# Output projections in 64x128 array tiles over four banks, and context values of both batches at once

## The chip, the cores and the metric

The kernel runs on one core of a Trainium2 chip. The metric is the device time of one launch in microseconds (us). A core has a matrix engine (TensorE, PE in the profile, with PEld for its weight loads), a vector engine (VectorE, DVE), an activation engine (ScalarE, ACT), a general one (GpSimd, POOL) and a queue that issues transfers (SyncE, SP). Each works through its own list of instructions in order and waits on semaphores for the others. PE writes into PSUM, eight banks of 128 rows by 512 fp32 numbers, and the other engines have to empty them.

## The reference

A transformer block on `x` (2 batches, 1024 tokens, 256 features) with a context of 2 x 154 rows of 192 features, all in fp32:

```
h = layernorm(x, ln1);  x = x + attention(h, h, sa_*)        # 16 heads of 64
h = layernorm(x, ln2);  x = x + attention(h, context, ca_*)  # 154 keys
h = layernorm(x, ln3);  p = h @ ff_w1 + ff_b1
x = x + (p[:, :1024] * gelu(p[:, 1024:])) @ ff_w2 + ff_b2
```

`attention` projects queries, keys and values to 1024 features, takes a softmax over the keys, weighs the values and projects the result back to 256 features with `wo`, adding `bo`.

## The kernel before

The work is cut into units: a unit is one batch and one pair of heads (8 pairs, 16 units a stage). There are three stages. Self-attention runs over 128 positions, eight a unit. The context stage ("ca", the loop `for c in range(CA)`) runs over 48 steps, three a unit: the counter `n` is 0, 1, 2, and a step handles 3, 3 and 2 tiles of 128 tokens. Steps are counted from 0, so that step 10 is n = 1 of unit 3. The feed-forward follows. Nothing is reordered behind the program: the order in which the code emits instructions is the order of each engine.

A step of the context stage does this. `cross_first` has PE compute the scores `sc` of its token tiles (K is 64, so the two heads of a pair run in the two row halves of the array) and DVE their negated maxima `neg`. ACT takes exponentials with their sums, three for each head in a step of three tiles. One step later, DVE takes reciprocals `rden` and POOL multiplies. Two steps later (`cross_drain`), DVE transposes the result into `pT_ca`.

Beside this, each n has its own work:

- n = 0: `cross_values` weighs the context values for the unit two before, over all four free banks (`poc`). DVE and ACT copy them out into `o_ca`, DVE's part emitted ahead of its transposes.
- n = 1: `cross_queries` projects the queries `pq_ca` of the next unit into the two main banks; ACT copies them out at the next step.
- n = 2: output projection, context values, and one turn of a norm.

The eight banks are four for scores (two buffers of two), two main ones (`mm_tile`) and two for sums (`sum_tile`). Each of the two small pools hands its banks out in turn.

The output projection takes two head pairs (`HP`) at a time, a group; a batch has four groups. `out_piece` computes two token tiles in one bank with full-array matmuls (`py_ca`, `py_sa`), and DVE adds them to `x`. Four pieces make a group. They are kept in `outs` and taken by `run_work`. Self-attention already uses another form, `out_rounds`: four token tiles in four banks. Each K of 128 is split into its two row halves, which run at once into two different banks and are then exchanged. Before the exchange ACT reads one element of a bank (`seen`) so that both halves are through. There the matmuls are cut into 64x32 tiles. The last self-attention group falls into the context stage and goes by `out_piece`.

The norms of the next stage are prepared beside. `norm_beside` puts pieces into `side`: pieces of statistics, deviation and normalization (DVE `st_ln`, `mv_ln`, `off_ln`; POOL `rstd_ln`, `xn_ln`) alternate with pieces of a turn, four transposes on PE (`ph_ln`) that DVE or ACT then stores into `home`. A turn needs a bank. `run_work` takes the pieces in their order and stops at a turn when it has no bank to give; it had one at n = 2 only. Context-attention's norm of batch 1 turns in units 3 to 6, the feed-forward's norm of batch 0 in units 12 to 15.

`context_values` computes the 128 first context rows' values for one batch and two head pairs: two fp32 matmuls with 96 rows each (an fp32 matmul is two instructions in the trace), an ACT copy into `own_v`, and a transfer to DRAM and back that spreads them to four partition groups (`vd`). It is called for even units, eight times.

Of the kernel before, what the change touches and what calls it, by code (L numbers as in the profile page):

```python
# [18 lines left out]
def tile_transformer_block(ctx: ExitStack, tc: tile.TileContext, a: dict, out: bass.AP):  # L19
# [127 lines left out]
    def load_weights(kind, pr, what):  # L147
        if kind == "sa" and what == "v":
            wsl[kind, pr, what], parts = load_slice(f"{kind}_w{what}", pr * P, VC, HR)
            return parts  # L150
        elif kind == "sa" or what == "q":
            wsl[kind, pr, what] = load_slice(f"{kind}_w{what}", pr * P, P, HR)
        elif pr % 2 == 0:
            wsl[kind, pr, what] = load_slice(f"{kind}_w{what}", pr * P, VC, CC)

# [379 lines left out]

    def out_rounds(b, g, tiles):

        o = oT["sa", b, g]
# [20 lines left out]
        def add(at):  # L559
            t = tiles[at]  # L560
            xs = xt[b, t // GT][:, t % GT, :]
            nc.vector.tensor_tensor(xs, py[at][:, :D], xs, ALU.add)
            added.add(("sa", b, g, t))

        for pair in range(2):
            cross(pair, 0)
        return [lambda pair=pair: second(pair) for pair in range(2)], [
            lambda at=at: add(at) for at in range(4)]

    def out_order(kind):  # L570
# [237 lines left out]

    held, kept, rounds = [], [], []

    def self_beside(ui):
# [15 lines left out]
        if ui >= HP and ui % HP == 0:  # L827
            ob, og = divmod(ui // HP - 1, NQ)
            for t0 in range(0, NG * 2, 2):
                rounds.append(  # L830
                    (ob, og, [t + e for t in out_order("sa")[t0:t0 + 2] for e in range(2)]))
        if ui in (4, 6):
            add_biases("sa", (ui - 4) // 2)

    coming, ahead_ends = [], []
    to_dram = [(1, 3), (1, 6), (3, 3)]
    from_dram = [(NU - 1, n) for n in (0, 3, 5)]

    def load_ahead(p):
# [17 lines left out]
        if ahead_ends and (ui == 1 and n == SH + 1 or ui == 2 and n in (0, 1, SH)):  # L857
            ahead_ends.pop(0)()
        if (ui, n) in to_dram:
            i = 2 * to_dram.index((ui, n))  # L860
# [92 lines left out]

    def context_values(b, pr, bank=mm_tile):

        v = vs["ca", b, pr // 2] = pt_.tile([P, NB, VC], F32, tag="V", name=f"v_ca{b}_{pr}")
        pv = bank(f"pv_ca{b}_{pr}")
        for c in range(2):  # L960
            nc.tensor.matmul(
                pv[:, :VC], lhsT=ctxT[:, c, b * TP:b * TP + P],
                rhs=wsl["ca", pr, "v"][:, c, :], start=(c == 0), stop=(c == 1),
            )

        def store():
            own = one.tile([P, VC], F32, tag="own_v", name=f"own_v{b}_{pr}")
            nc.scalar.copy(own, pv[:, :VC])
            later.insert(0, lambda: nc.sync.dma_start(out=vd[b, pr][:P, :], in_=own))

            def back(a0):
                for a4 in range(a0, a0 + 2):
                    nc.sync.dma_start(
                        out=v[a4 * KB:(a4 + 1) * KB, :, :],
                        in_=vd[b, pr].rearrange("(n p) d -> p n d", p=KB))

            later.insert(2, lambda: back(0))
            later.insert(3, lambda: back(2))

        return store  # L980
# [8 lines left out]
    def cross_first(c):  # L989
# [18 lines left out]

        def then(between=None):
            pr_ = pp_.tile([P, 2, TG, NB * KB], F32, tag="P", name=f"p_{c}")  # L1010
            nc.gpsimd.memset(pr_[:, :, :, T:], 0.0)
            den = small.tile([P, 2, TG], F32, tag="den", name=f"den_{c}")
            for j in range(2):
                if j and between:
                    between()
                for i in range(nt):
# [62 lines left out]
    def cross_beside(ui):  # L1079
# [3 lines left out]
        if ui > HP and ui % HP == 1:  # L1083
            out_pieces("ca", *divmod(ui // HP - 1, NQ), out_order("ca"))
        if ui == NU - 5:
# [238 lines left out]
    with tc.manual_schedule():  # L1324
# [53 lines left out]
        side.append((True, (), lambda: together(*(lambda b=b: turn_context(b) for b in range(B)))))  # L1378
        side.append((True, (), turn_rows))
        work.append(costing(2, lambda: self_queries(*units[0], P, 2 * P)))  # L1380
        work.extend(value_pieces(0, (mm_tile, sum_tile)))
        work.append(costing(2, lambda: three_keys(0)))

        for p in range(SA):
# [23 lines left out]
            if p < 2 * SH - 1 or p % SH in (1, 2):  # L1408
# [9 lines left out]
                elif p == SA - 2:  # L1418
                    hold_late_keys()
                    run(lambda: context_values(*units[0]))  # L1420
                    for pr in range(NKD, NPAIR):
# [7 lines left out]
        for c in range(CA):  # L1429
# [5 lines left out]
            if c == SH:  # L1435
                out_pieces("sa", B - 1, NQ - 1, out_order("sa"))
# [4 lines left out]
            ui, n = divmod(c, len(CG))  # L1441
            nxt = units[ui + 1] if ui + 1 < NU else None
            if n == 0:
# [3 lines left out]
            elif n == 2 and nxt and ui:  # L1447
                load_weights("ca", nxt[1], "v")
            flush(adds)
            between = None  # L1450
            if c < 2:
# [5 lines left out]
            if c < 2:  # L1457
                weighted(SA + c - 2, 0)
                weighted_beside(SA + c - 2, 1)
                if c == 0:  # L1460
                    slot[SA - 1]["dd"] = differences(SA - 1, slot[SA - 1]["st"])
                    between = lambda: softmax_join(SA - 1)
# [134 lines left out]
```

## Time and profile before

| | us |
|---|---|
| median of 3 runs | 1060.7 (1059.21 to 1061.69) |
| the profiled execution | 1060.44 |
| its span | 1058.6 |
| PE busy | 1047.1 |
| DVE busy | 880.7 |
| POOL busy | 769.9 |
| ACT busy | 658.9 |
| `py_ca`, 256 instructions | 61.1 |
| `pv_ca`, 32 instructions | 8.5 |

A row of the timeline is start, length, engine, line, operation, out<-in, shape and count. In a matmul's shape "64*128" is the tile of the array, "64x256" rows by moving columns. Matmuls are pipelined, so that the length of one is more than its distance to the next. A row of groups ends with busy time, the mean of one in ns, and the engine's idle time ahead of it with what ended it. A row of stretches gives for PE, PEld, DVE, ACT and POOL the busy time and the count, then the granted clock of PE, the share of the DMA engines and GB/s.

### The profile page before, as it was taken

The page shows a single profiled execution, that of the slowest core. Times are in us where ns is not written, and L with a number is a line of the kernel's source. Part 1 is how long each engine was busy: PE and PEld are TensorE (multiplying, and loading weights), DVE is VectorE, ACT ScalarE, POOL GpSimd, SP SyncE. Part 2 cuts the span into 40 slices and gives each one's busy share as a digit, 9 for nine tenths or more (in the row PEclk, how much of TensorE's full clock was granted, in tenths as well). Part 3 has the DMA queues.
Part 4 walks back from the last instruction along what each step waited for, and adds up shares of the span by engine and source line. Part 5 has one row for each costly group of instructions (what it writes and reads, how often), then busy time and mean ns, then how long its engine had stood idle before and what let it go on. Part 6 is the DMA issues. An engine that isn't in the chain of part 4 may idle for free.

```text
span 1058.6 us, 51303 instructions
## 1 busy us (share of the span) xinstructions
PE 1047.1 (99%) x21700; PEld 740.3 (70%) x21700; DVE 880.7 (83%) x1313; ACT 658.9 (62%) x2147; POOL 769.9 (73%) x1620
## 2 busy tenths in 40 slices
PE   8999999999999999999999999999999999999998
PEld 6456965556576666665786676666676667889997
DVE  5799999999899999999999999968776777675654
ACT  5776767777776766766776777666666655243221
POOL 2677777788778777777777777757665777598773
PEclk9999999999999999999999999999999999999999
DMA  4322221121121021122122012135323221000000
GB/s 106 95 65 60 50 61 42 45 54 34 25 54 45 15 54 45 29 44 55 24 44 50 21 39 56 49 104 132 101 59 83 69 59 41 1 11 11 21 11 30
DMA packets 96023, 52.87 MB, mean 50 GB/s; under 512 B 30314, under 2 KB 93810, under 8 KB 95794
## 3 DMA queue, kind: packets, MB, share of 16 engines
q1 hardware_dynamic: 94466, 48.93, 18.9%
q8 instruction: 171, 2.80, 1.1%
q10 hardware_dynamic: 1328, 0.66, 0.2%
q14 instruction: 58, 0.48, 0.1%
HBM read 36.23 MB, written 4.39 MB: 38 GB/s over the span
## 4 chain that ended last, share of the span: by engine, by line
PE 90%; DVE 4%; ACT 2%; POOL 2%; issue 1%; DMA 1%; SPq 0%; DVEq 0%; POOLq 0%; ACTq 0%
PE s L583 20%; PE po L639 20%; PE pv_sa L443 5%; PE py_ca L523 5%; PE pk_sa L411 5%; PE pq_sa L411 5%; PE pr L547 5%; PE pf L1289 5%; PE poc L1064 4%; PE pb L1169 4%; PE pq_ca L411 4%; PE sc L999 3%; PE pa L1169 2%; PE pc L1169 2%; PE ph_ln L323 1%
## 5 line engine op out<-in xcount | busy, mean ns | idle before, releaser
L600 ACT ACTIVATE p<-s,st 128x512 f32<-128x512 f32 x512 | 345.4, 685 | 152.8 <-DVE st L592 121.4
L706 POOL TENSOR_SCALAR p<-p,rd,ee 128x512 f32<-128x512 f32 x508 | 385.2, 768 | 75.5 <-DVE rd L698 75.1
L592 DVE TENSOR_REDUCE st<-s 128x2 f32<-128x1024 f32 x256 | 308.7, 1207 | 49.9 <-issue 16.1
L733 DVE STREAM_TRANSPOSE pT<-p 128x1024 f32<-128x1024 f32 x256 | 303.9, 1221 | 2.4 <-POOL p L706 2.3
L583 PE MATMUL s<-k_sa,q_sa 64*32 64x512 f32 x4096 | 256.7, 590 | 1.1 <-DVE k_sa L432 0.6
L639 PE MATMUL po<-pT,v_sa 64*32 64x256 f32 x6144 | 180.5, 376 | 1.7 <-ACT p L1017 1.6
L639 PEld LDWEIGHTS po<-pT,v_sa 64*32 64x32 f32 x6144 | 142.7, 106 | 45.0 <-issue 15.2
L583 PEld LDWEIGHTS s<-k_sa,q_sa 64*32 64x32 f32 x4096 | 102.8, 106 | 78.5 <-issue 51.4
L1017 ACT ACTIVATE p<-sc,neg 128x154 f32<-128x154 f32 x256 | 97.1, 406 | 72.2 <-DVE rden L1025 70.2
L1028 POOL TENSOR_SCALAR p<-p,rden 128x154 f32<-128x154 f32 x256 | 96.8, 399 | 52.9 <-DVE rden L1025 51.9
L600 ACT ACTIVATION_READ_ACCUMULATOR p<-s,st 128x1 f32 x512 | 103.0, 201 | 0.0
L1004 DVE TENSOR_REDUCE neg<-sc 128x6 f32<-128x924 f32 (+1 forms) x48 | 48.1, 1003 | 20.2 <-PE sc L999 20.0
L523 PE MATMUL py_ca<-ca_wo,o_ca 128*128 128x256 f32 x256 | 61.1, 385 | 0.0
L639 PE MATMUL po<-pT,third_v 64*32 64x256 f32 x2048 | 60.5, 376 | 0.0
L443 PE MATMUL pv_sa<-sa_wv,home 64*32 64x256 f32 x2048 | 60.2, 376 | 0.0
L443 PEld LDWEIGHTS pv_sa<-sa_wv,home 64*32 64x32 f32 x2048 | 48.4, 106 | 14.1 <-issue 5.4
L411 PE MATMUL pq_sa<-home,sa_wq 64*32 64x512 f32 (+1 forms) x976 | 58.0, 586 | 0.0
L411 PE MATMUL pq_ca<-home,ca_wq 64*128 64x512 f32 (+1 forms) x352 | 57.8, 589 | 0.0
L639 PEld LDWEIGHTS po<-pT,third_v 64*32 64x32 f32 x2048 | 46.6, 106 | 16.0 <-issue 4.6
L1017 ACT ACTIVATION_READ_ACCUMULATOR p<-sc,neg 128x1 f32 x256 | 56.5, 221 | 0.0
L627 POOL TENSOR_TENSOR zz<-ee,st 128x8 f32<-128x8 f32 x128 | 25.8, 202 | 42.1 <-ACT ee L625 42.1
L411 PE MATMUL pk_sa<-home,sa_wk 64*32 64x512 f32 x960 | 56.3, 589 | 0.0
(144 smaller groups left out, 1576.1 us busy)
## 6 DMA issues: line engine op xcount, KB each, us to landing
st<-st SPq DMA_DIRECT2D x510, 1.0 KB, 1.7
v_sa<-v_sa SPq DMA_DIRECT2D x24, 256.0 KB, 3.3
v_ca<-vd SPq DMA_DIRECT2D x32, 160.0 KB, 3.4
sa_wq<-in_L_xattn_sa_wq_dram SPq DMA_DIRECT2D x32, 128.0 KB, 3.3
sa_wk<-in_L_xattn_sa_wk_dram SPq DMA_DIRECT2D x32, 128.0 KB, 3.1
sa_wv<-in_L_xattn_sa_wv_dram SPq DMA_DIRECT2D x32, 128.0 KB, 3.3
ca_wq<-in_L_xattn_ca_wq_dram SPq DMA_DIRECT2D x32, 128.0 KB, 3.0
wf<-in_L_xattn_ff_w_dram SPq DMA_DIRECT2D x12, 256.0 KB, 4.8
```

Source lines behind the costliest of these rows:

```text
L411: nc.tensor.matmul(pq[r][f:f + m, at:at + n], lhsT=wt[own, c, f:f + m], rhs=h[own, c, t0:t0 + n], start=(c == 0), stop=(c == NH - 1), tile ...
L443: nc.tensor.matmul(pv[r][f:f + KB, i * VC:(i + 1) * VC], lhsT=h[own, c, t0:t0 + KB], rhs=wt[own, c, :], start=(c == 0), stop=(c == NH - 1) ...
L523: nc.tensor.matmul(py[:, e * D:(e + 1) * D], lhsT=o[:, i, (t + e) * P:(t + e + 1) * P], rhs=wo[kind, b, g][:, i, :], start=(i == 0), stop= ...
L583: nc.tensor.matmul(sc[a4 * KB:(a4 + 1) * KB, j, :], lhsT=q[r, c:c + KB], rhs=k[r, h * HB:(h + 1) * HB], start=True, stop=True, tile_positi ...
L592: nc.vector.tensor_reduce(st[:, 0, 0, i, :], sc, AX.X, ALU.max, negate=True)
L600: nc.scalar.activation(pr[:, j, :], sc[:, j, :], AF.Exp, bias=st[:, 0, 0, i, j:j + 1], accum_out=st[:, 0, 1, i, j:j + 1],)
L639: nc.tensor.matmul(po[a2][d:d + KB, :QH // 2], lhsT=v[r, t, e, d:d + KB], rhs=pT[r, d // DH * NK + n, :], start=(t == 0 and e == 0), stop= ...
L706: nc.gpsimd.tensor_scalar(pr[:, j, :], pr[:, j, :], v["rd"][:, c:c + 1], v["ee"][:, 0, c:c + 1], op0=ALU.mult, op1=ALU.mult,)
L733: nc.vector.transpose(halves[h][:, :, c:c + KB], slot[p]["members"][i].rearrange("p j (n k) -> p (j n) k", k=KB))
L1017: nc.scalar.activation(pr_[:, j, i, :T], sc[:, j, i * T:(i + 1) * T], AF.Exp, bias=neg[:, j, i:i + 1], accum_out=den[:, j, i:i + 1],)
L1028: nc.gpsimd.tensor_scalar(pr_[:, j, i, :T], pr_[:, j, i, :T], rden[:, j, i:i + 1], 1.0, op0=ALU.mult, op1=ALU.mult,)
L1169: nc.tensor.matmul(into[:, :BT], lhsT=lhs, rhs=wh[pair][i], start=first, stop=True, skip_group_check=True)
```

## The change

- `out_rounds` serves both kinds of attention and takes the tile width `m`. The last group of self-attention and all groups of context attention but the last go by rounds with 64x128 tiles. A round runs at n = 2 (at n = 1 too in units 1 and 15), between the scores and the exponentials; ACT's two `seen` reads stand ahead of the exponentials of the first and of the second head. Its four adds go to DVE at the start of the next step.
- The turn of a norm runs at n = 1, between the scores and the queries, in a sum bank. Pieces without a turn still run at n = 0.
- `context_values` handles both batches: the context is copied (eight transfers during self-attention) into `ends`, batch 0 in rows 0 to 63 and batch 1 in rows 64 to 127, three chunks of 64; the weights are loaded into both halves of the rows. It runs at n = 1 of units 2, 4 and 6 in two sum banks, and once at the end of self-attention in two main banks. Batch 1 loads no value weights and no longer projects; it fetches its spread values.
- `poc` takes the sum banks first in some units.

```diff
-    def out_rounds(b, g, tiles):
+    def out_rounds(kind, b, g, tiles, m=KB):
...
-                for f in range(0, P, KB):
+                for f in range(0, P, m):
                     for r in (1, 0):
                         at = 2 * pair + (r ^ swapped)
                         own, t0 = slice(r * HR, (r + 1) * HR), tiles[at] * P + f
                         nc.tensor.matmul(
-                            py[at][f:f + KB, :D], lhsT=o[own, i, t0:t0 + KB],
-                            rhs=wo["sa", b, g][own, i, :],
+                            py[at][f:f + m, :D], lhsT=o[own, i, t0:t0 + m],
+                            rhs=wo[kind, b, g][own, i, :],
...
+    def four_by_four(kind, b, g):
+
+        pairs = out_order(kind)
+        for i in range(0, len(pairs), 2):
+            rounds.append((kind, b, g, [t + e for t in pairs[i:i + 2] for e in range(2)]))
...
+    def context_values(pr, bank):
+        v = hold_values(0, pr)
+        pv = [bank(f"pv_ca{b}_{pr}") for b in range(B)]
+        for c in range(DC // HR):
+            for b in range(B):
+                own = slice(b * HR, (b + 1) * HR)
+                nc.tensor.matmul(
+                    pv[b][:, :VC], lhsT=both_ctx[own, c, :], rhs=wsl["ca", pr, "v"][own, c, :],
+                    start=(c == 0), stop=(c == DC // HR - 1), tile_position=(b * HR, 0))
...
             if n == 0 and ui > 1:
-                own, between = cross_values(ui - 2, [mm_tile] * 2 + [sum_tile] * 2)
-                lates.append(then(between))
+                banks = [mm_tile] * 2 + [sum_tile] * 2
+                if side and side[0][0] or ui % 2 == 0 and not b:
+                    banks.reverse()
+                own, copy = cross_values(ui - 2, banks)
+                lates.append(then([copy]))
                 own()
             else:
+                if n == 1 and ui:
+                    spare["turned"] = True
+                    if ui % 2 == 0 and not b:
+                        run(lambda: context_values(ui, sum_tile))
+                    run_work(0, 1, sum_tile)
+                    flush(stores)
+                if rounds and (n == 2 or n == 1 and (ui == 1 or not nxt)):
+                    between, taken = out_rounds(*rounds.pop(0), P)
                 lates.append(then(between))
...
             elif n == 1:
-                spare["turned"] = True
-                if ui == 1 or not nxt:
-                    run_work(2, 0)
-                else:
+                if ui > 1 and nxt:
                     run(lambda: cross_queries(*nxt))
-                run_work(0, 1)
             else:
-                run_work(0, 0, n_sum=1)
-                flush(adds)
-                if ui and ui % 2 == 0:
-                    run(lambda: context_values(*units[ui]))
-                run_work(0, 1, mm_tile)
-                flush(stores)
-                if ui > 1:
-                    run_work(0, 0, n_sum=1)
+                if b and ui % 2 == 0:
+                    hold_values(*units[ui])
+                    spread_values(*units[ui], 0)
...
+            adds.extend(taken)
```

More of the change, by code (lines that the diff above doesn't have):

```diff
@@ L153, in load_weights @@
         elif pr % 2 == 0:
-            wsl[kind, pr, what] = load_slice(f"{kind}_w{what}", pr * P, VC, CC)
+            t = wsl[kind, pr, what] = wpool.tile(
+                [P, DC // HR, VC], F32, tag="wv", name=f"{kind}_w{what}_{pr}")
+            own = w[f"{kind}_w{what}"][:, pr * P:pr * P + VC].rearrange("(c p) f -> p c f", p=HR)
+            for r0 in range(0, P, HR):
+                nc.sync.dma_start(out=t[r0:r0 + HR], in_=own)
     def load_ahead_parts():
@@ L807, in self_first @@
         return then
[L809 removed]
+    held, kept = [], []
     def self_beside(ui):
@@ L828, in self_beside @@
             ob, og = divmod(ui // HP - 1, NQ)
-            for t0 in range(0, NG * 2, 2):
-                rounds.append(
-                    (ob, og, [t + e for t in out_order("sa")[t0:t0 + 2] for e in range(2)]))
+            four_by_four("sa", ob, og)
         if ui in (4, 6):
@@ L952, in context_ends @@
         return store
[L954 to L964, printed above, removed]
-        def store():
[L967 to L978, printed above, removed]
+    both_ctx = ends[:, :DC // HR * P].rearrange("p (c k) -> p c k", k=P)
@@ new lines, in context_beside @@
+    def context_beside():
+        moves = []
+        for b in range(B):
+            for c in range(DC // HR):
+                f = c * HR
+                while f < (c + 1) * HR:
+                    half, row = divmod(f, CC)
+                    n = min((c + 1) * HR - f, CC - row)
+                    to = b * HR + f - c * HR
+                    moves.append(lambda b=b, c=c, half=half, row=row, n=n, to=to: nc.sync.dma_start(
+                        out=both_ctx[to:to + n, c, :],
+                        in_=ctxT[row:row + n, half, b * TP:b * TP + P]))
+                    f += n
+        return moves
@@ new lines, in hold_values, with spread_values, back @@
+    def hold_values(b, pr):
+        v = vs["ca", b, pr // 2] = pt_.tile([P, NB + B, VC], F32, tag="V", name=f"v_ca{b}_{pr}")
+        return v
+    def spread_values(b, pr, at):
+        def back(a0):
+            for a4 in range(a0, a0 + 2):
+                nc.sync.dma_start(
+                    out=vs["ca", b, pr // 2][a4 * KB:(a4 + 1) * KB, :NB, :],
+                    in_=vd[b, pr].rearrange("(n p) d -> p n d", p=KB))
+        later.insert(at, lambda: back(0))
+        later.insert(at + 1, lambda: back(2))
@@ L1007, in cross_first, with then @@
         )
-        def then(between=None):
+        def then(between=()):
             pr_ = pp_.tile([P, 2, TG, NB * KB], F32, tag="P", name=f"p_{c}")
@@ L1013, in then @@
             for j in range(2):
-                if j and between:
-                    between()
+                for fn in between[j:j + 1] if len(between) > 1 else between if j else ():
+                    fn()
                 for i in range(nt):
@@ L1419, in tile_transformer_block @@
                     hold_late_keys()
-                    run(lambda: context_values(*units[0]))
+                    run(lambda: context_values(0, mm_tile))
                     for pr in range(NKD, NPAIR):
@@ L1447, in tile_transformer_block @@
             elif n == 2 and nxt and ui:
-                load_weights("ca", nxt[1], "v")
+                if not nxt[0]:
+                    load_weights("ca", nxt[1], "v")
             flush(adds)
-            between = None
+            between, taken = (), ()
             if c < 2:
```

24 lines of the change are left out of this document (19 added, 5 removed).

## The prediction

> **What bounds the kernel now.** I read the page first, then busy time by stretch, then the timeline of single units in the context stage.
>
> ```profile
> span 1058.6 us, 51303 instructions
> PE 1047.1 (99%) x21700; PEld 740.3 (70%) x21700; DVE 880.7 (83%) x1313; ACT 658.9 (62%) x2147; POOL 769.9 (73%) x1620
> PE   8999999999999999999999999999999999999998
> PEclk9999999999999999999999999999999999999999
> PE 90%; DVE 4%; ACT 2%; POOL 2%; issue 1%; DMA 1%; SPq 0%; DVEq 0%; POOLq 0%; ACTq 0%
> ```
> ```profile
> 760.00:820.00 60.00, 60.00 (x726) 43.13 (x724) 42.77 (x86) 37.54 (x175) 36.36 (x102) 1.00 0.32 81
> ```
>
> The edits act in the context stage (687 to 892 us, 16 units of three steps). There the columns of the second fence (PE, PEld, DVE, ACT, POOL) give PE 60.00 of 60 and DVE 42.77: every microsecond that PE waits is lost, every one of PE work saved is won. The other engines have time to spare, but each runs in order, so what matters is how soon after PE they finish.
>
> **The projections themselves.**
>
> ```profile
> 736.46 1.89 PE L523 MATMUL py_ca<-ca_wo,o_ca 128*128 128x256 f32 x8
> 19.59 2.00 PE L411 MATMUL pq_sa<-home,sa_wq 64*128 64x256 f32 x16
> L961 PE MATMUL pv_ca<-ca_wv,ctxT 96*128 96x256 f32 x32 | 8.5, 388 | 0.3 <-ACT q_ca L426 0.2
> ```
>
> A full-array matmul instruction costs (1.89-0.386)/7 = 0.215 us, 0.386 being the length of one. In 64x128 tiles two run at once: (2.00-0.376)/7.5 = 0.217 us a pair, of which about 0.1 in all is the change of tile shape ahead of it. A round of 16 fp32 matmuls (32 instructions) is 16 pairs, 3.46 us, exactly what its two old pieces took. The new shape by itself gives **0**.
>
> Context values: before, 8 calls of 4 instructions (32 in the row), 8 x 0.86 = 6.9 us. After, 4 calls of 12 instructions, 6 pairs each, 4 x 1.30 = 5.2. **-1.7**.
>
> **Changes of tile shape.**
>
> ```profile
> 785.18 0.69 PE L999 MATMUL sc<-k,q_ca 64*128 64x154 f32 x8
> 785.80 3.72 PE L523 MATMUL py_ca<-ca_wo,o_ca 128*128 128x256 f32 x16
> 789.45 0.79 PE L999 MATMUL sc<-third_v,q_ca 64*128 64x154 f32 x8
> ```
>
> From 785.18 to 789.45 are 4.27 us; 4 score pairs of 0.13 and 16 x 0.216 are 3.98. Another 0.10 lies in the scores behind (0.79 against 0.69 for the same eight). So entering and leaving the full-array shape cost 0.39, about 0.195 each. Before, 17 blocks of pieces make 33 such changes (the last runs into poc, which changes shape anyway). After, only the 8 turns of the norms do, 16. 17 x 0.195: **-3.3**.
>
> **Waits that go.**
>
> ```profile
> PEld pv_ca L961 <- ACT q_ca L426: 1.1, 2, 0.6
> PE ph_ln L323 <- ACT q_ca L426: 0.3, 1, 0.3
> ```
>
> Two old context-value calls and one turn found their main bank still full of queries. Of the first row I count 0.7 as lost by PE (the rest ran beside matmuls), with the second **-1.0**; bounds 0.3 and 1.4. Both now write sum banks, where no queries lie.
>
> The last pieces of self-attention become two rounds in unit 1, with the same 6.9 us of work. The first writes sum banks that self-attention's own sums have just left:
>
> ```profile
> 707.03 1.06 PE L999 MATMUL sc<-third_v,q_ca 64*128 64x154 f32 x12
> 707.14 0.65 ACT L771 COPY o_sa<-po 128x256 f32<-128x256 f32 x2
> ```
>
> ACT has copied them at 707.79, PE is there at 708.01 or a tenth sooner: 0. If that cover went (ACT late by one exponential, 0.4), it would cost 0.4 once.
>
> **The turn is moved one step forward: the main term.** The turn (ph_ln) of a norm used to run in step n = 2, from a main bank. Now it runs in n = 1, between the scores and the queries (pq_ca), from a sum bank. What makes its operand (statistics, off_ln, xn_ln) stays in n = 0. In the built order unit 3's turn of xn_ln_1_0 stands in step 10 and its off_ln at the end of DVE's step 9; units 4, 5, 6 and 12 to 15 are alike. Unit 4 before shows when that operand is done:
>
> ```profile
> 738.28 1.06 PE L999 MATMUL sc<-third_v,q_ca 64*128 64x154 f32 x12
> 739.26 2.41 PE L1064 MATMUL poc<-pT_ca,v_ca 32*64 32x256 f32 x80
> 741.61 1.06 PE L999 MATMUL sc<-third_v,q_ca 64*128 64x154 f32 x12
> 741.68 0.76 DVE L1075 COPY o_ca<-poc 128x256 f32<-128x256 f32 x2 [1.10 <-PE poc L1064]
> 742.36 1.23 DVE L1044 STREAM_TRANSPOSE pT_ca<-p 128x480 f32<-128x480 f32 x2
> 742.50 3.60 PE L411 MATMUL pq_ca<-home,ca_wq 64*128 64x512 f32 x16
> 743.51 0.39 DVE L266 BATCH_NORM_STATS2 st_ln<-x 128x6 f32<-128x256 f32 x1
> 744.55 0.13 DVE L290 SCALAR_TENSOR_TENSOR off_ln<-mv_ln,rstd_ln 128x2 f32<-128x2 f32 x1
> 744.79 1.08 POOL L310 TENSOR_SCALAR xn_ln<-x,rstd_ln,off_ln 128x256 f32<-128x256 f32 x2 [1.47 <-DVE off_ln L290]
> ```
>
> DVE can only begin its part when poc ends, at the start of the n = 1 scores: copies, transposes, statistics, off_ln; then POOL's two xn_ln end at 745.87, **4.26** after the scores' start. Nothing of this chain is changed. PE arrives at the turn 0.98 after the scores' start (they take as long from 738.28 to poc at 739.26, also a change of shape). PE is in order, so pq_ca and all behind it wait. Units 5 and 15 show the chain without statistics, and the start of the program the lag from operand to turn:
>
> ```profile
> 755.26 1.06 PE L999 MATMUL sc<-third_v,q_ca 64*128 64x154 f32 x12
> 757.39 1.09 POOL L310 TENSOR_SCALAR xn_ln<-x,rstd_ln,off_ln 128x256 f32<-128x256 f32 x2 [0.42 <-DVE off_ln L290]
> 882.09 1.06 PE L999 MATMUL sc<-k,q_ca 64*128 64x154 f32 x12
> 884.22 1.08 POOL L310 TENSOR_SCALAR xn_ln<-x,rstd_ln,off_ln 128x256 f32<-128x256 f32 x2 [1.46 <-DVE off_ln L290]
> 11.20 0.55 POOL L310 TENSOR_SCALAR xn_ln<-x,rstd_ln,off_ln 128x256 f32<-128x256 f32 x1 [0.56 <-DVE off_ln L290]
> 11.88 0.63 PE L323 MATMUL ph_ln<-ident,xn_ln 128*128 128x128 f32 x4 [0.15 <-POOL xn_ln L310]
> ```
>
> xn_ln ends 3.22 and 3.21 after the scores' start there; the lag is 11.88-11.75 = 0.13. After the change statistics stand ahead of off_ln in units 3, 4, 12 and 13, and not in 5, 6, 14 and 15 (eight tiles, two a piece). Units 3, 12, 13: 4.26+0.13-0.98 = 3.41 each. Units 5, 14, 15: 3.22+0.13-0.98 = 2.37 each. In units 4 and 6 the context values stand ahead of the turn and fill 1.30: 2.11 and 1.07. Together 10.2+7.1+3.2 = **+20.5**. Less only if the chain got shorter: the low end takes half, 10. Not below, since the turn truly reads xn_ln.
>
> In unit 15 a round follows the turn directly and its first matmul writes the sum bank that the turn just filled. DVE must store it first: two of
>
> ```profile
> L334 DVE TENSOR_SCALAR home<-ph_ln,cols 128x256 f32<-128x256 f32 x8 | 4.0, 537 | 1.2 <-PE ph_ln L323 1.2
> ```
>
> or 1.07, and about 0.15 of latency: **+1.2**.
>
> **A round takes all four free banks.** Its second pair goes into the main banks, which hold the queries until ACT has copied them. Unit 9 before, where the pieces used sum banks only:
>
> ```profile
> 809.89 0.69 PE L999 MATMUL sc<-third_v,q_ca 64*128 64x154 f32 x8
> 810.87 1.11 ACT L426 ACTIVATE q_ca<-pq_ca 128x512 f32<-128x512 f32 x2
> L562 DVE TENSOR_TENSOR x<-pr,x 128x256 f32<-128x256 f32 x56 | 21.0, 395 | 0.0
> L556 ACT COPY seen<-pr 1x1 f32<-1x1 f32 x28 | 3.7, 132 | 0.0
> ```
>
> The copies end 2.09 after the scores' start. PE has done scores (0.53) and the first half of pair 0 (0.86) at 1.39 and waits about 0.7, with latency 0.77. Units 7 to 11 are like this: 5 x 0.77, **+3.9**. Units with a turn escape: while PE waits for xn_ln, ACT catches up. If it escaped everywhere, 0. The "seen" reads (0.13 each, on ACT between PE's halves) then come in time: the first at 2.24, PE wants it at 3.0. The four adds of a round (4 x 0.395 against 2 x 0.68 before) run ahead of the next reduce; the last ends some 0.95 after the round, poc wants its bank at 0.87: 0.1 in some 10 units, **+1.0**, bounds 0 and 3. The eight moves of the context into `ends` and the extra out-and-back transfers stand on SP's queue; DMA is 0.32 busy, PE waits for none of them, and batch 1's value weights are no longer loaded: 0, at most 1 if a weight tile lands late.
>
> The Trainium skill speaks against this edit (TensorEngine Tiling (Array Packing), Gotcha 1: PSUM Pressure): row tiles must write to different banks, and software has to synchronize them. Taken to hold in every context round, 14 x 0.77 = 10.8 would stand for the 3.9 and the sum would end at 1088 (an estimate); unit 9's rows show the wait, the turns' rows why it should not be general.
>
> **The sum** against the profiled execution: -1.7-3.3-1.0+20.5+1.2+3.9+1.0 = +20.6. Span 1058.6 to 1079.2, time 1060.44 to 1081.0; the median of the runs shown is 0.3 higher, and I say **1081**.
>
> **Rivals.**
> - *Half the wait* (15%): something ahead of off_ln shortens, as DVE's transposes moving behind it would. +10 in place of +20.5: 1071. Against it: DVE's built order has them ahead.
> - *The turn does not wait* (5%): only if xn_ln were done by 0.98. Then -6.0+3.9+1.0, or with the bank's 1.2, about 0: 1060 to 1062. No unit shows xn_ln earlier than 3.2.
> - *Row halves run faster than the full array* (3%), the one that ends below: 16 rounds are 256 pairs. At 0.215-20.6/256 = 0.135 a pair it would break even, at half the price it would save 27: 1054. The pq_sa row (0.217) speaks against it.
> - *The clock drops in the waits* (7%):
>
> ```profile
> L1351 PE MATMUL first<-ident 128*128 128x128 f32 x27 | 5.0, 369 | 1.9 <-POOL ident masks.py:199 1.9
> L323 PE MATMUL ph_ln<-ident,xn_ln 128*128 128x128 f32 x96 | 15.0, 279 | 2.0 <-POOL xn_ln L310 1.8 <-ACT q_ca L426 0.3
> ```
>
> The first transposes after the idle start last 369 ns, the same shape later 279. If PE came out of the three waits of 3.4 us that slowly, 3.5 us of queries each at up to twice the time would add 10: 1091. The Trainium skill (TensorE: Matmul & The Clock Gate, Part 1) puts the drop to half clock at an idle window of about 3.4 us; no run here shows a gap that long.
>
> **How the numbers follow.** The forecast has 70%, the rivals 15, 5, 3 and 7. The range 1071 to 1090 holds the forecast with its bounds and the half wait. Less than 0.2% (2 us) is about what a measurement of this kernel can't tell from no change: faster 4% (the third rival and a sliver of the second), same 3%, slower 93%.
>
> **What would show it.** In the profile after: PE below 60 of 60 in stretches of 700 to 820; ph_ln of the context stage with idle ahead, released by POOL xn_ln, 1 to 3.4 us, eight times; units 3, 12, 13 longer by about 3; pr pairs 0.216 apart; pr released by ACT q_ca in units 7 to 11; no gap in the self-attention stage. Wrong would be: xn_ln ending less than 2 us after the n = 1 scores, or poc, not the turn, carrying the waits.

## The result, and the profile after

The changed kernel takes 1091.2 us (median of 5 runs, 1089.5 to 1092.7) against 1060.7 for the kernel before in the same comparison: a ratio of 1.0284, with an interval of 1.0266 to 1.0301. The prediction said 1081.0 and a range that ended at 1090. The direction and the main cause are as predicted; something of about 9 us came on top of them, which the prediction had listed as a rival with a chance of 7%.

The page of the profile after, the rows that answer to the ones of before:

```profile
span 1087.7 us, 51946 instructions
PE 1058.4 (97%) x21972; PEld 749.6 (69%) x21972; DVE 884.2 (81%) x1345; ACT 664.1 (61%) x2179; POOL 770.2 (71%) x1620
...
PE   8999999999999999999999999989899889999998
...
PEclk9999999999999999999999999998999998999999
```

Two things are new. PE, at nine tenths everywhere but at the ends before, has slices of eight in the context stage. And the granted clock, nine tenths or more in every slice before, is at eight in two of them (27 and 33, at 734 and 897 us): something slowed PE itself.

The context stage from its first scores to the first `pa` of the feed-forward can be read as one stretch. First the kernel before, then the kernel after (start and end, length, then PE, PEld, DVE, ACT, POOL busy with their counts, granted clock, DMA share, GB/s):

```profile
687.57:893.88 206.31, 204.16 (x2644) 145.80 (x2636) 153.29 (x321) 126.42 (x585) 144.15 (x380) 1.00 0.32 83
```
```profile
687.58:923.03 235.45, 214.46 (x2908) 157.26 (x2901) 157.57 (x353) 131.36 (x616) 144.21 (x380) 0.96 0.30 72
```

The stage begins at the same time and is 29.1 us longer; what follows it, up to the end of the span, takes 164.7 in both. PE's idle time grew from 2.15 to 20.99, which is 18.8. PE's busy time grew too, by 10.3, although there is less work to do, and the clock in the stage is 0.96. So the loss has two parts of different kinds: PE stands still for some 19 us, and PE runs slowly for some 10.

Where it stands still is told by PE's waits in the context stage of the kernel after (total, times, longest):

```profile
PE ph_ln L327 <- POOL xn_ln L314: 17.3, 12, 3.3
...
PE pr L551 <- ACT q_ca L430: 1.1, 1, 1.1
```

The turn waits for its operand, as forecast. Unit 4 after, for comparison with unit 4 before:

```profile
744.20 2.53 PE L1109 MATMUL poc<-pT_ca,v_ca 32*64 32x256 f32 x80
...
746.62 0.76 DVE L1120 COPY o_ca<-poc 128x256 f32<-128x256 f32 x2 [1.09 <-PE poc L1109]
...
746.66 1.06 PE L1044 MATMUL sc<-third_v,q_ca 64*128 64x154 f32 x12
...
747.55 1.46 PE L1012 MATMUL pv_ca<-ca_wv,ends 64*128 64x256 f32 x12
...
749.73 1.08 POOL L314 TENSOR_SCALAR xn_ln<-x,rstd_ln,off_ln 128x256 f32<-128x256 f32 x2 [1.46 <-DVE off_ln L294]
...
750.87 0.66 PE L327 MATMUL ph_ln<-ident,xn_ln 128*128 128x128 f32 x4 [1.86 <-POOL xn_ln L314]
...
751.46 5.40 PE L415 MATMUL pq_ca<-home,ca_wq 64*128 64x512 f32 x16
```

The scores start at 746.66 and `xn_ln` ends at 750.81, 4.15 later (4.26 forecast). PE stands idle for 1.86 in front of the turn although the context values filled a part of the wait. The last row is the surprise: the 16 query instructions take 5.40 where the same 16 took 3.60 before.

### The profile page after: what moved, and what is told of

It reads as the page before. It is cut to its first block, busy times and chain, and to the rows that moved or that the text cites. A ratio compares the mean times of both kernels' runs of the same rounds, so it can differ in the third digit from the quotient of the medians.

```text
span 1087.7 us, 51946 instructions
## 1 busy us (share of the span) xinstructions
PE 1058.4 (97%) x21972; PEld 749.6 (69%) x21972; DVE 884.2 (81%) x1345; ACT 664.1 (61%) x2179; POOL 770.2 (71%) x1620
## 3 DMA queue, kind: packets, MB, share of 16 engines
q1 hardware_dynamic: 94978, 49.13, 18.7%
## 4 chain that ended last, share of the span: by engine, by line
PE 85%; DVE 5%; POOL 3%; ACT 2%; issue 2%; DMA 1%; SPq 1%; DVEq 0%; POOLq 0%; ACTq 0%
PE po L651 19%; PE s L595 19%; PE pr L551 10%; PE pv_sa L447 5%; PE pk_sa L415 4%; PE pf L1334 4%; PE pq_sa L415 4%; PE pq_ca L415 4%; PE pb L1214 3%; PE poc L1109 3%; PE pa L1214 2%; PE pc L1214 2%; PE sc L1044 2%; DVE pT_ca L1089 1%; ACT p L1062 1%
## 5 line engine op out<-in xcount | busy, mean ns | idle before, releaser
L415 PE MATMUL pq_ca<-home,ca_wq 64*128 64x512 f32 (+1 forms) x352 | 65.3, 636 | 0.0
L566 DVE TENSOR_TENSOR x<-pr,x 128x256 f32<-128x256 f32 x120 | 45.3, 408 | 18.4 <-PE pr L551 12.9
L551 PE MATMUL pr<-ca_wo,o_ca 64*128 64x256 f32 x448 | 58.8, 398 | 1.5 <-ACT q_ca L430 1.1
L551 PE MATMUL pr<-sa_wo,o_sa 64*32 64x256 f32 (+1 forms) x1856 | 59.7, 377 | 0.0
L551 PEld LDWEIGHTS pr<-sa_wo,o_sa 64*32 64x32 f32 (+1 forms) x1856 | 46.2, 109 | 15.5 <-issue 5.5
```

Source lines behind the costliest of these rows:

```text
L415: nc.tensor.matmul(pq[r][f:f + m, at:at + n], lhsT=wt[own, c, f:f + m], rhs=h[own, c, t0:t0 + n], start=(c == 0), stop=(c == NH - 1), tile ...
L551: nc.tensor.matmul(py[at][f:f + m, :D], lhsT=o[own, i, t0:t0 + m], rhs=wo[kind, b, g][own, i, :], start=swapped == 0 and i == 0, stop=swap ...
```

## The experiments

The runs below were made in three groups on three chips; each ratio is to the kernel before on the same chip, where its median was 1062.2 to 1063.1 (the row of the changed kernel is the first comparison, against 1060.7). On one of them that kernel was profiled again:

> The kernel before, unchanged, profiled on this chip, to see where its stages begin and end here. The self-attention stage began the context stage at 687.6 in the first profile; the kernels run so far on this chip began it at 690.5 to 693.5. If that is the chip: the same here, 689 to 693, and a time of 1061 to 1064. If it comes from the change: 687 to 688.

```profile
690.38:896.68 206.30, 204.18 (x2645) 145.78 (x2637) 153.30 (x321) 126.40 (x585) 144.13 (x380) 1.00 0.32 83
```

It took 1063.2. The context stage starts 2.8 later than in the first profile and is 206.30 long, against 206.31. So the start differs by chip and run (689.0 to 693.5 in all runs of these groups) and does not come from the change, as the first of the two readings had it, and the length of the stage can be compared to a tenth. It stands beside each ratio below.

| kernel | ratio to before [interval] | stage, us | PE idle in it |
|---|---|---|---|
| before | 1 | 206.3 | 2.1 |
| changed | 1.0284 [1.0266, 1.0301] | 235.5 | 21.0 |
| fill in the waits | 1.0197 [1.0180, 1.0213] | 226.0 | 6.6 |
| half the fill | 1.0222 [1.0202, 1.0241] | 227.6 | 13.2 |
| statistics first | 1.0178 [1.0163, 1.0194] | 224.9 | 15.5 |
| norm earlier | 1.0065 [1.0050, 1.0080] | 211.0 | 7.3 |
| norm earlier, full array | 1.0041 [1.0027, 1.0055] | 210.1 | 5.9 |
| norm earlier, reduce first | 1.0012 [1.0000, 1.0024] | 207.0 | 5.0 |
| the same, turns in a main bank | 1.0025 [1.0015, 1.0034] | 208.0 | 3.8 |
| waits mended | 1.0008 [0.9999, 1.0017] | 206.8 | 4.8 |
| waits mended, full array | 1.0019 [1.0010, 1.0028] | 207.9 | 3.9 |

**Is it the gaps that slow PE?** The theory: the turn's wait costs about 19, and the gaps it leaves bring half the clock afterwards. Busy work in the gap keeps the wait and removes the gap.

```diff
+            if spare["turned"]:
+                many = {"ca": (26, 12, 16, 5), "ff": (22, 22, 13, 13)}[kind][t // 2]
+                for _ in range(many):
+                    nc.tensor.transpose(ph[0][:, :P], ident, ident)
```

> Adds work to the changed kernel: ahead of the transposes of each turn in the context stage PE transposes a constant 128x128 tile into the same bank (5 to 26 times, as long as that turn waited), and the turn then overwrites it. So PE is busy while xn_ln is late, but reads xn_ln no sooner. Theory (the waits cost about 19 us, and the gaps in them drop the granted clock afterwards for about 10 more): no record of half the clock in the context stage, the queries' pairs back from 840 to about 430 ns, the turns still as late: 1079 to 1083, 8 to 12 less than the changed kernel's 1091. Rival 1 (the clock drops for another reason than the gaps, the power drawn for one): the records stay and the time with them, 1090 to 1094. Rival 2 (the clock's drop is only seen in the records and costs no time): no record, but 1090 to 1092.

Unit 3 of this kernel, PE's rows:

```profile
735.13 3.06 PE L328 MATMUL ph_ln<-ident 128*128 128x128 f32 x26
738.48 0.65 PE L331 MATMUL ph_ln<-ident,xn_ln 128*128 128x128 f32 x4 [0.29 <-POOL xn_ln L314]
739.06 3.70 PE L419 MATMUL pq_ca<-home,ca_wq 64*128 64x512 f32 x16
```

The whole stage of this kernel:

```profile
692.55:918.58 226.03, 219.47 (x3037) 166.10 (x3029) 157.33 (x353) 131.25 (x616) 144.79 (x380) 1.00 0.31 75
```

The turn is as late as it was, the queries behind it are back at 3.70, and the stage has the clock 1.00. It is 9.4 shorter than that of the changed kernel (235.5 to 226.0). PE did more work and the kernel became faster; the ratio is 1.0197. So 9.4 is the price of the slow clock, and it hangs on the gaps; both rivals are out.

**How long must a gap be?** The prediction had thought of three waits of 3.4. Two runs shorten the gaps in different ways: one emits the norm's pieces ahead of DVE's transposes, the other halves the fill (its edit is shown against the kernel with the fill).

```diff
+            if c > 3 and n == 0:
+                run_work(0, 1)
             cross_drain(c)
...
             elif n == 0:
-                run_work(0, 1)
+                pass
```

> The changed kernel, with the norm's pieces at n = 0 emitted ahead of DVE's transposes of that step, so that off_ln is 1.23 us earlier and the turn's position on PE is the same. It shortens the waits without removing them: from 3.4 to about 2.2 in units 3, 12 and 13, by less in the others, where POOL's own row sets xn_ln. Theory A (half the clock needs an idle stretch of about 3.4 us at once): all records of half the clock go, waits shorter by 5 to 6: 1075 to 1078. Theory B (half the clock comes after a fixed window of 3.41 us in which PE was idle for more than about half, 1.5 to 1.8 us): one to three records stay, depending on how the waits lie against the windows: 1077 to 1084.

```diff
-                many = {"ca": (26, 12, 16, 5), "ff": (22, 22, 13, 13)}[kind][t // 2]
+                many = {"ca": (13, 6, 8, 2), "ff": (11, 11, 6, 6)}[kind][t // 2]
```

> The changed kernel with half as many extra transposes ahead of the turns as in the first of these runs (2 to 13), so that PE idles for half of each wait: 1.6 to 2 in units 3, 12 and 13, about 1 in the others. If half the clock follows a window of 3.41 us that is idle for more than half (1.7), at most one or two records stay, and the time is 1084 (that of the full fill) to 1088. If any wait above 1 us brings it, all records stay, 1091 to 1093.

In the first of them the waits shrink (waits of PE in the context stage):

```profile
PE ph_ln L327 <- POOL xn_ln L314: 10.6, 11, 2.5
```

From 17.3 to 10.6 in all, and the stage is 224.9, which is 10.6 less: part of it waits, part clock. Three records of half the clock are left in the stage, in place of five; with half the fill one is left, and the stage is 1.5 longer than with the whole fill. All records start on one grid of 3.41 us (in the kernel after 735.08 and 752.14 are five steps apart), so the question can be put to each window of the grid. Windows of the kernel after, in pairs, each with the one that follows it:

```profile
731.67:735.08 3.41, 1.61 (x10) 0.97 (x12) 2.56 (x8) 1.71 (x9) 2.65 (x6) 1.00 1.11 220
735.08:738.49 3.41, 3.41 (x12) 1.39 (x10) 1.27 (x4) 0.63 (x4) 2.15 (x6) 0.50 0.68 159
748.73:752.14 3.41, 1.55 (x12) 0.87 (x10) 2.52 (x9) 2.04 (x10) 2.31 (x5) 1.00 0.42 114
752.14:755.55 3.41, 3.41 (x12) 1.39 (x10) 1.60 (x5) 0.94 (x6) 2.48 (x7) 0.50 1.04 248
765.79:769.20 3.41, 1.99 (x12) 1.12 (x14) 2.59 (x9) 2.27 (x14) 3.04 (x8) 1.00 0.00 0
769.20:772.61 3.41, 3.41 (x28) 2.16 (x25) 1.43 (x4) 1.30 (x4) 0.38 (x2) 1.00 0.00 0
875.02:878.43 3.41, 1.04 (x6) 0.69 (x8) 2.63 (x9) 1.22 (x8) 1.87 (x4) 1.00 0.77 171
878.43:881.84 3.41, 3.41 (x10) 1.39 (x10) 1.68 (x4) 1.50 (x9) 3.02 (x8) 0.50 0.00 0
```

PE was busy for 1.61, 1.55 and 1.04 us of the windows ahead of the ones at clock 0.50, and 1.99 ahead of one at 1.00. A window that is busy for less than about half is followed by a window at half the clock. In the context stages of all runs half the clock followed 0.94 to 1.72 us of busy time every time, and it did not come after 1.75 to 2.04, with three exceptions: with half the fill it came after 1.82, with the statistics first after 2.18, and in the kernel after it stayed on for a second window in unit 15:

```profile
905.74:909.15 3.41, 1.60 (x17) 1.02 (x14) 2.63 (x7) 1.47 (x8) 1.88 (x5) 1.00 0.00 0
909.15:912.56 3.41, 3.28 (x13) 2.29 (x15) 1.79 (x4) 0.15 (x2) 3.41 (x10) 0.50 0.00 0
912.56:915.97 3.41, 3.41 (x19) 2.93 (x17) 0.63 (x2) 2.41 (x13) 0.29 (x1) 0.50 0.00 0
```

The ends of matmuls are modelled in the trace, and a matmul that waits can show as busy, which may account for the three; that stays open. So does the exact border: behind the last matmuls of the program, in two of the runs, the window after one of 1.68 was still at the full clock. Theory A (3.4 us at once) is out, for PE's idle time in unit 4 was 1.86, and with the statistics first no wait for `xn_ln` is longer than 2.5 while three records stay. Theory B holds but for its exact border. Unit 5 shows the other side of it: its wait (2.23) is longer than that of unit 4 (2.02), but it falls into two windows, the later of which is the one of 1.99 above, and the clock stays full. With the statistics first the wait of unit 5 is shorter, 1.86, but leaves PE busy for only 1.72 of one window, and half the clock follows there.

**Is it the turn's wait that bounds all the rest?** Statistics, `off_ln` and `xn_ln` are made two steps earlier, by letting pieces without a turn run at n = 2 as well. PE's order stays.

```diff
             else:
+                run_work(0, 1)
                 if b and ui % 2 == 0:
```

> The changed kernel, with pieces of a norm that need no bank also run at n = 2, so that statistics, off_ln and xn_ln are made two steps ahead of the turn that reads them; PE's order is the same. Theory (the turn's wait for xn_ln is the main term, and the clock hangs on it): ph_ln has no idle time ahead in the context stage, no record of half the clock, and about 29 of the 30.5 us go: 1060 to 1064. What is left by the prediction's sum: -6.0 for the work saved, +1.2 for the bank in unit 15, +2 to +6 for the wait of a round's second pair for the copies of the queries (more units have it once no turn gives ACT time), +1.0 to 1.5 for poc. Rival (the rounds and not the turns carry the loss; the turn's wait only hides a wait that comes anyway): pr or poc show the idle time in its place, 1075 to 1090.

The stage of this kernel, and PE's waits in it:

```profile
690.48:901.46 210.98, 203.71 (x2908) 152.73 (x2900) 156.96 (x353) 130.54 (x616) 146.12 (x382) 1.00 0.34 81
```
```profile
PE pr L551 <- DVE home L338: 1.7, 1, 1.7
...
PE pr L551 <- ACT q_ca L430: 1.1, 1, 1.1
PE ph_ln L327 <- ACT v_ca L1021: 1.1, 2, 0.5
PE ph_ln L327 <- POOL xn_ln L314: 0.9, 1, 0.9
```

The clock is 1.00, of twelve waits for `xn_ln` one is left, and 24.5 of the 29.1 are gone. That is less than expected: the ratio of 1.0065 is 6.9 us, where 3 at most were expected. The list names what stood behind the turn's wait. In units 4 and 6 the turn now waits for a bank, since the context values still hold both sum banks (`v_ca`); in unit 15 the round waits 1.7 for the turn's bank; unit 3 still waits 0.9 for the norm's first `xn_ln`. The rival (the rounds carry the loss) has these few us and no more.

**The queries' copies.** In the units without a turn a round's second pair waits for ACT. DVE's transposes of n = 0 are put behind the reduce of n = 1, so that everything behind the maxima comes earlier.

```diff
-            cross_drain(c)
+            if n or ui < 2:
+                if n == 1 and ui > 1:
+                    cross_drain(c - 1)
+                cross_drain(c)
```

> The kernel with the norm's pieces also at n = 2, and besides DVE's transposes of n = 0 postponed to n = 1 behind the reduce of that step, so that the maxima, the exponentials and ACT's copies of the queries behind them come about 1.2 us earlier. Theory (the second pair of a round waits for the queries' copies, which hang on the reduce): pr released by ACT q_ca loses its idle time, 2 to 4 us less than the kernel with the norm's pieces alone, 1057 to 1062. Rival (ACT is late for another reason, or DVE's transposes now come too late for poc of the next unit): the same or 1 to 5 more, with poc released by DVE pT_ca.

Unit 9, first of the changed kernel, then of this one:

```profile
822.32 0.69 PE L1044 MATMUL sc<-third_v,q_ca 64*128 64x154 f32 x8
822.84 4.23 PE L551 MATMUL pr<-ca_wo,o_ca 64*128 64x256 f32 x31
826.83 0.29 PE L1044 MATMUL sc<-third_v,q_ca 64*128 64x154 f32 x1
...
823.28 1.11 ACT L430 ACTIVATE q_ca<-pq_ca 128x512 f32<-128x512 f32 x2
```
```profile
817.78 0.69 PE L1044 MATMUL sc<-third_v,q_ca 64*128 64x154 f32 x8
818.31 3.69 PE L551 MATMUL pr<-ca_wo,o_ca 64*128 64x256 f32 x32
821.77 0.49 PE L1044 MATMUL sc<-third_v,q_ca 64*128 64x154 f32 x4
...
817.98 1.11 ACT L430 ACTIVATE q_ca<-pq_ca 128x512 f32<-128x512 f32 x2
```

The copies of the queries start 0.20 after the scores and not 0.96, and from these scores to the next are 3.99 and not 4.51. The stage lost 4.0 against the kernel with the norm earlier, the top of what was expected; the ratio is 1.0012.

**What the 64x128 tiles are worth.** The full array in the rounds, all else as in the kernel with the norm earlier:

```diff
         def cross(pair, swapped):
+            if m == P:
+                at = 2 * pair + swapped
+                for i in range(HP):
+                    nc.tensor.matmul(
+                        py[at][:, :D], lhsT=o[:, i, tiles[at] * P:(tiles[at] + 1) * P],
+                        rhs=wo[kind, b, g][:, i, :], start=i == 0, stop=i == HP - 1)
+                return
```

> The kernel with the norm's pieces also at n = 2, with one thing undone: in the 16 rounds of 64x128 tiles each token tile is again one full-array product (K of 128 at once) into one bank, over the same four banks and at the same places. It tests two terms of the prediction: that the row halves cost what the full array costs (0), and that changes of tile shape cost about 0.195 each. If both hold: the rounds' own matmuls take the same 3.46 each, and 16 blocks with an entry and an exit come back, 16 x 0.39 = 6.2 less what the waits for the queries' copies hide of it (up to 0.5): 1075 to 1077 against 1070. If the changes of shape cost nothing: 1070. If the row halves were the slower form (as the exchange and its waits might make them): below 1070.

This missed: 0.9 less in the stage (and 1.0041 against 1.0065), not 5 to 7 more. The round at the end of unit 14, full array first, then row halves (the kernel with the norm earlier):

```profile
879.72 0.69 PE L1051 MATMUL sc<-k,q_ca 64*128 64x154 f32 x8
880.34 3.72 PE L549 MATMUL pr<-ca_wo,o_ca 128*128 128x256 f32 x16
883.99 0.80 PE L1051 MATMUL sc<-k,q_ca 64*128 64x154 f32 x8
```
```profile
880.17 0.69 PE L1044 MATMUL sc<-k,q_ca 64*128 64x154 f32 x8
880.69 3.67 PE L551 MATMUL pr<-ca_wo,o_ca 64*128 64x256 f32 x32
884.15 0.60 PE L1044 MATMUL sc<-k,q_ca 64*128 64x154 f32 x6
```

Where nothing waits, the round is shorter with row halves: 3.98 from scores to scores against 4.27, which is 0.29, and the scores behind it reach `poc` in 0.92 against 0.99. The products themselves are 0.216 apart in both forms, so this is the change of shape, 0.36 a round and close to the 0.39 of the prediction. But the row halves give it back in two places. Their tiles are done and added later, so that in the kernel with the norm earlier the weight loads of `poc` wait for the adds 13 times, and with the full array never:

```profile
PEld poc L1109 <- DVE x L566: 2.1, 13, 0.2
```

By the starts of its instructions `poc` takes 32.3 in the stage and not 30.8, and whole units without another wait (5, 6 and 14) differ by 0.23 only. And in units 8 to 10, where the second pair waits for the queries, the unit is 0.29 longer with row halves (12.35 against 12.06), 0.09 of it from scores to scores and 0.20 in the scores behind. A pair in row halves writes both main banks at once and so needs both copies of the queries. Unit 9 of the kernel with the norm earlier, the weight loads of the round and the two copies:

```profile
817.61 0.29 PEld L551 LDWEIGHTS pr<-ca_wo,o_ca 64*128 64x128 f32 x2 [0.48 <-ACT q_ca L430]
818.09 2.02 PEld L551 LDWEIGHTS pr<-ca_wo,o_ca 64*128 64x128 f32 x19 [0.19 <-ACT seen L560]
...
816.93 1.11 ACT L430 ACTIVATE q_ca<-pq_ca 128x512 f32<-128x512 f32 x2
```

The loads for the first bank start 0.05 behind the first copy (it ends at 817.55), those for the second bank 0.05 behind the second (818.04; the `seen` read that the row names ends at the same time, but by the order of the program it belongs to the exchange, which comes later). So the row halves lose 0.38 between their instructions after the stop. The full array fills one bank after the other, does not wait for the second copy, and loses 0.10.

**Mending the waits.** Two further kernels tried to get what the sum promised once the turn is out of the way. The first gives the turn a main bank where its sum bank was taken:

```diff
-                    run_work(0, 1, sum_tile)
+                    run_work(0, 1, sum_tile if nxt and (ui % 2 or b) else mm_tile)
```

> The kernel with the norm's pieces also at n = 2 and DVE's transposes of n = 0 behind the reduce of n = 1, and besides the turn of units 4, 6, 12, 14 (batch 0's even ones by their number) and 15 taken from a main bank instead of a sum bank where it collided: in units 4 and 6 with the context values, which still held both sum banks (0.7 each), in unit 15 with the round's first bank (about 1.3). Theory: these three waits go, 2.7 less: 1060 to 1063 on this chip, a tie with the kernel before or up to 0.3% better. Rival: the queries now wait for the store of the turn's main bank, pq_ca released by DVE home, and nothing is won.

In this kernel's stage:

```profile
PE pq_ca L415 <- DVE home L338: 0.8, 2, 0.4
```

Only units 4, 6 and 15 got a main bank (12 and 14, which the expectation names too, did not). The rival came true in units 4 and 6, each 0.8 longer than with the sum bank: the queries use both main banks at once and wait for the store. Unit 15 gained 0.9. The last kernel keeps what had won (shown against the changed kernel), and its twin puts the full array back:

```diff
-                    run_work(0, 1, sum_tile)
+                    run_work(0, 1, sum_tile if nxt else mm_tile)
...
-            cross_drain(c)
+            plain = ui in (2, 7, 8, 9, 10, 11)
+            if n or not plain:
+                if n == 1 and plain:
+                    cross_drain(c - 1)
+                cross_drain(c)
...
             else:
+                run_work(0, 1)
                 if b and ui % 2 == 0:
```

> The changed kernel with all that the runs so far showed to win: the norm's pieces also at n = 2; DVE's transposes of n = 0 behind the reduce of n = 1, but only in the units without a turn (2 and 7 to 11), since in units 3, 4 and 12 that order cost 0.15 to 0.35 each; and the turn of unit 15 alone in a main bank (0.9). From the traces: the context stage up to the first pa was 206.3 before and 207.0 with the reduce first; 207.0 - 0.7 - 0.9 = 205.4. So 0.9 less than the kernel before, a ratio of 0.998 to 1.001: what the change saves (6.0 in the prediction's sum) is nearly all spent on the waits that are left (poc for the adds, two turns for the banks of the context values, unit 3's turn for xn_ln).

> The same kernel with the full array in the rounds again, one product for each token tile. With the second pair's wait for the queries' copies mostly gone, it shows what the 64x128 tiles are worth by themselves. By the prediction (0.39 for an entry and an exit in 16 rounds): 6.2 slower than the row halves. By units 5, 12 and 14 of the full-array run (0.23 each): 3.5 slower. If the row halves were worth nothing: the same.

The first is at 206.8 and not 205.4, level with the kernel before (1.0008): units 3, 4 and 12 did not come down, and in unit 15 the wait only moved to the round's second pair.

```profile
887.26 2.61 PE L551 MATMUL pr<-ca_wo,o_ca 64*128 64x256 f32 x21 [0.84 <-DVE home L338]
```

The twin is 1.1 longer, less than both estimates. Units 5 to 10 and 14 are 0.20 to 0.24 longer each and unit 1 with its two rounds 0.45, so the saving of the row halves is there; but unit 15, where the round waits, is 1.3 shorter with the full array. Within the units `poc` moves the other way, 33.1 with the row halves and 31.4 with the full array. No version was faster than the kernel before.

## Why the prediction was wrong, step by step

The mechanism was right, and the forecast failed at one step: *the clock drops in the waits* was set beside the forecast as a rival, at 7%, where it is a consequence of the forecast itself. Its condition was taken to be waits of 3.4 us, and the reason given against it was that no run showed a gap that long, although the forecast's own main term makes three of them. The runs show that a window of 3.41 us need only be less than about half busy, which waits of 2 us reach if they fall into one window. The forecast with its own waits of 3.4, three times over, should have had the clock inside the sum. The price set on it (10) came close to the 9.4 measured, but by luck. It stood for three stretches of 3.5 us of queries at half speed. The runs show six windows in five units: four of them stretch the queries of units 3, 4, 12 and 13 from 3.54 to 5.23, 1.70 each and 6.8 in all, and two lie one behind the other in unit 15, for which 2.6 is left.

By terms, for the stage of 206.3 that became 235.5 (+29.1), read from the starts of PE's instructions:

| term | predicted | measured |
|---|---|---|
| the turn waits for `xn_ln` | +20.5 | +19.4 |
| half the clock behind it | 0 (rival: +10) | +9.4 |
| second pair waits for the queries, units 7 to 11 | +3.9 | +4.1 |
| unit 15, the turn's bank | +1.2 | about +1.2 |
| `poc` waits for the adds | +1.0 | +0.3 |
| unit 2's scores wait for ACT, unit 1's round for `seen` | 0 | about +0.9 |
| context values, tile shapes, old waits | -6.0 | -6.2, what is left over |

- *The turn.* 3.43 in unit 3 (3.41 predicted), 2.02 in unit 4 (2.11), 2.23 in unit 5 (2.37), 1.03 in unit 6 (1.07), and 19.4 with units 12 to 15. There the turn starts with the first of two `xn_ln` and waits again for the second, which takes a little off. These waits are counted from 0.89 after the scores' start, the end of the scores ahead; by the 0.98 of the prediction, which has the change of shape in it, they are 0.7 less, 18.7, and the last row is -5.5. The chain of DVE and POOL, read from unit 4 before, carried over to a tenth.
- *The second pair.* The sum is right in part by luck: 0.5 in unit 7, 0.64 in 8 to 10, 1.7 in 11, against 0.77 each. Unit 11 is not like unit 9: there the first statistics of the feed-forward's norm stand ahead of the reduce on DVE (844.61 to 845.65 in the kernel after), and the copies start 2.00 after the scores and not 0.96. In the units with a turn there was none, as argued. The Trainium skill's rule that row tiles need different banks and that software has to order them (TensorEngine Tiling (Array Packing), Gotcha 1: PSUM Pressure), taken to cost a wait in every context round, would have been 10.8: the trace shows such waits in five units alone. The `seen` reads came in time but for unit 1, where the round takes 3.69 and not 3.46 and its last exchange waits for one.
- *The shapes.* -3.3 stood on 0.39 for entering and leaving. The full-array run gives 0.36 where nothing else waits (0.29 up to the next scores and 0.07 in them), so that the price was nearly right: 17 x 0.18 is 3.1. The remainder of -6.2 can't confirm it, as it also takes up the errors of all other rows.
- *`poc`.* It costs little as long as the turns hold PE up. Once they don't, it is 0.9 (norm earlier) to 1.9 (reduce first): another wait that stood behind the first, and one that row halves make longer, as their tiles are added later.
- *The rivals.* "Half the wait" and "does not wait" are out (`xn_ln` ended 4.15 after the scores in unit 4). "Row halves faster than the full array" is out: a round of 16 pairs that waits for nothing takes 3.46 from its first start to the next scores (880.69 to 884.15 above), the very price that was put on it.
- *The range.* It added nothing for forecast and clock together: 20.6 + 10 would have been 1091, which is where it came out, with the luck in the 10 told above.

## What to carry to other kernels

Before a step of PE is moved forward, ask when its operand is ready, in its own rows, and look at what stands in front of the instruction that makes it on the other engine's list: moving the producers two steps forward gave back 24.5 of 29.1 us here, with one line. If a change leaves PE idle for some 2 us in one place, price the slow clock behind the gap together with the wait and not as an alternative to it; here it was half the wait's own cost again. And a rearrangement that saves 6 us of a PE-bound stage is only worth what the next waits in line leave of it: after the mending it was a tie.

## What was not expected of the hardware

- Half the clock comes in whole windows of 3.41 us on a fixed grid, and it does not take an idle window: PE had been busy for 0.94 to 1.72 us of the window ahead in nearly all cases. The Trainium skill (TensorE: Matmul & The Clock Gate, Part 1) describes the window of 3413 ns that runs freely, which the grid of the records bears out; its idle state comes there after at least one idle window, and the measurement differs: about half a window without work was enough.
- Making PE do useless work in a gap it could not avoid made the context stage 9.4 us shorter. The work was transposes alone, and they kept the clock at 1.00.
